# An early-fusion model on one core: merged transfers, one second encoder layer for both halves, keys turned by narrow products, and fill products of 128 columns

## The chip, the cores and the metric

The kernel runs on one core of one Trainium2 chip. The metric is the device time of one execution in microseconds. Before the change three timed executions took 3369.94, 3370.55 and 3380.7 us, median 3370.55.

## What is computed

Sixteen images and sixteen texts go through a tokenizer, two layers and an LSTM, all in float32. Cut to its core:

```
h = tokenizer(x)                       # 2x2 convolution, attention over 441 tokens of 256
h = concat([h, txt])                   # 16 sequences x 569 positions x 256
h = h + window_attention(layernorm(h)) # shifted windows of 64, 8 heads
h = h + top2_experts(layernorm(h))     # 8 experts, 256 -> 512 -> 256, gelu
# layer 1, attention: x = layernorm(h)
kp = tanh(gelu(x @ Wk1 + bk1) @ Wk2 + bk2) * freq * pi   # 64 key phases
qp = tanh(gelu(x @ Wq1 + bq1) @ Wq2 + bq2) * freq * pi   # 64 query phases
V  = x @ Wv + bv
memory    = cumsum(exp(i*kp)[..., None] * V[:, :, None, :], axis=1)
retrieved = real(sum(memory * exp(-i*qp)[..., None], axis=2)) / sqrt(pos * 64)
h = h + layernorm(retrieved) @ Wo + bo
# layer 1, feed-forward: y = layernorm(h)
xp = y @ W_ih.T + b_ih + b_hh
for t in range(569):
    gates = xp[:, t] + h_t @ W_hh.T;  i, f, g, o = split(gates)
    c = sigmoid(f) * c + sigmoid(i) * tanh(g);  h_t = sigmoid(o) * tanh(c)
# a gated prefix and suffix sum over the states, added to h
```

The LSTM's 569 steps depend on each other; nothing of one step can start before the state of the step before.

## The kernel before

**First part (0 to about 950 us).** Tokenizer, window attention and routing run as interleaved streams. Rows are normalised, routed, and scattered into `XS` by indirect DMAs (`send`, L904-916), two for each chunk of 128 rows. The list of places `at` (L899) stands in the pool `wk` of this part.

**Expert stage (about 950 to 1577 us).** `experts` (L1090-1265) computes which expert each of 79 tiles of 256 rows belongs to (`where`, L1139 and L1149). `weights` (L1165) loads an expert's packed weights (1154 KB) and `load` (L1171) the rows `xs`; the first two tiles' weights are issued ahead of everything (`ahead`, just below). Both stand in the pool `mo`. Four streams of tiles share TensorE. Beside them `prepare` (L1001-1077) loads what the next stage needs and clears buffers, among them the two `XO` buffers on GpSimd (L1044).

**Flow stage (about 1577 us to the end).** The sequence is cut into 10 blocks: one of 32 positions, eight of 64, one of 25 (`BLOCKS`). `fronts` and `backs`, two streams each, prepare the input of the LSTM, always two pairs of sequences a stream:

- `front` (L1340): adds the experts' rows to `h`, normalises, turns it, the encoders' first layers (`ek`, `eq`), the values `v`, and the encoders' second layer `z`. `Wk2` and `Wq2` are held twice side by side (`l1["Wk2"]`, [128, 2, 2, 64]), so that a product yields the 64 phases twice, in rows 0-63 (for the cosine) and 64-127 (for the sine). There are 36 fronts.
- `back` (L1474): scores `sc` of keys with queries, the keys turned by a whole-array transpose (L1490), `r` = retrieved, `ds` = what is added to the state, the output product `po`, the rows stored to `HF` (L1571), and the input projection `xm` with `Wih`, whose result `xp` is stored to `XCD` (three gates) and `XOD` (output gate) in DRAM (L1596, L1600). There are 36 backs with scores' turning and 4 late ones.

The steps of the recurrence (`steps`, L1661) read those stores back: `load` (inside it, L1671) fetches a unit of 8 positions, one DMA for `XC` and four for the four quarters of `XO`, each into 16 of the 32 rows of a quarter; the other 16 rows stay zero. A step then is: copy of the input into the PSUM banks `gates` and `out_gate` (L1690, L1695), products with `W_hh` (L1741, L1750), tanh of the gates (L1762, L1770), clearing the banks by a product of zeros (L1684), cell and state on VectorE (L1777 to L1805), tanh of the cell (L1798). `all_sums` does the prefix sums behind it.

**What sets the order.** Every f32 product of the fill work goes through `product`, which cuts the 128 output rows into four products of 32 rows[...]:

```
for m in range(0, out.shape[0], 32):
    own = slice(m, min(m + 32, out.shape[0]))
    nc.tensor.matmul(out[own], lhsT[:, own], rhs, start=start, stop=stop)
```

The order of TensorE, VectorE, ScalarE and GpSimd is written out while the program is built, by a planner (class `Order`). Each stream yields pieces with an engine and a cost, such as `yield "PE", 256 * COLUMN` (0.43 us); the recurrence has a table of its own costs (`STEP`). At each point the planner takes the recurrence's next step or a piece of fill work that fits in front of it, with an allowance `spare` of 0 to 0.45 us that depends on how far the backs of the next block are. Each engine then runs its list in order. A block's load waits, in the planner and on the chip, for all four backs of that block. The DMAs of SP are not in this order: the framework places them.

Of the kernel before, what the change touches and what calls it, by code (L numbers as in the profile page):

```python
# [10 lines left out]
F32 = mybir.dt.float32  # L11
BF16 = mybir.dt.bfloat16
AF = mybir.ActivationFunctionType
# [37 lines left out]
STEPS = 8  # L51
# [48 lines left out]

UNITS = np.arange(D).reshape(4, 2, 32).transpose(1, 0, 2).reshape(-1)
# [13 lines left out]
TURN = 0.11  # L115
# [179 lines left out]
def kernel(ctx: ExitStack, tc: tile.TileContext, a: dict, out: bass.AP):  # L295
# [489 lines left out]
    def routing():  # L785

        for p, lo, hi in PARTS:
# [111 lines left out]
            at = wk.tile([128, 2, n], mybir.dt.int32, name=f"at{u}", tag="at", bufs=3)  # L899
# [53 lines left out]
    XOD = [dram.tile([4, NB, n, 64], F32, name=f"XOD{j}") for j, (_, n) in enumerate(BLOCKS)]  # L953
# [35 lines left out]
    for n in ("Wk2", "Wq2"):  # L989
        l1[n] = l1w.tile([128, 2, 2, 64], F32, name=n)  # L990
# [10 lines left out]
    def prepare(mo):  # L1001
# [3 lines left out]
        def kxn(n):  # L1005
            return a[n].rearrange("(k p) n -> p k n", p=128)
# [9 lines left out]
        for n in ("Wk2", "Wq2"):  # L1016
            for i in range(2):
                nc.sync.dma_start(l1[n][:, :, i, :], kxn(n))
# [25 lines left out]
        for t in XO:  # L1044
            yield "POOL", 0.5
            nc.gpsimd.memset(t.rearrange("p t x -> p (t x)"), 0.0)
# [46 lines left out]
    def experts(g, mo, slots):  # L1093
# [71 lines left out]
        def weights(j, e=None):  # L1165
            e = planned(1, j, j + 1, E - 1)[0] if e is None else e
            w = mo.tile([128, WPACK], F32, name=f"w{g}_{j}", tag="w", bufs=bufs)
            nc.sync.dma_start(w, a["wpack"][bass.ds(e, 1)].rearrange("e p n -> (e p) n"))
            return w
# [169 lines left out]
    def front(p, c, n, at, slot):  # L1339
# [33 lines left out]
        for name in ("k", "q"):  # L1373
            e = bank(f"e{name}{u}", slot).rearrange("p (k n) -> p k n", k=2)
            g[name] = wk.tile([128, 2, 256], F32, name=f"g{name}{u}", tag=f"g{name}{slot}")
            for oc in range(2):
                for k in range(2):
                    yield "PE", 256 * COLUMN
                    product(
                        e[:, oc, :], l1[f"W{name}1"][:, k, oc * 128 : (oc + 1) * 128],  # L1380
                        xT[:, k, :], start=(k == 0), stop=(k == 1),
                    )
            for oc in range(2):
                yield "ACT", 0.46, "gelu"
                nc.scalar.activation(
                    g[name][:, oc, :], e[:, oc, :], AF.Gelu, bias=col(f"b{name}1", oc)
                )
# [8 lines left out]
        for j in range(2):  # L1396
            for k in range(2):
                yield "PE", 256 * COLUMN
                product(
                    v[:, j, :], xT[:, k, j * 128 : (j + 1) * 128], l1["Wv"][:, k, :],  # L1400
                    start=False, stop=(j + k == 2),
                )
        yield "DVE/ACT", 0.69, 0.58
        copy(V[:, both, :], v)
        z = bank(f"z{u}", slot).rearrange("p (k n) -> p k n", k=2)
        y = wk.tile([128, 2, 256], F32, name=f"fy{u}", tag=f"xn{slot}")
        for i, name in enumerate(("k", "q")):
            for k in range(2):
                yield "PE", 256 * COLUMN
                product(  # L1410
                    z[:, i, :], l1[f"W{name}2"][:, k].rearrange("p i x -> p (i x)"),
                    g[name][:, k, :], start=(k == 0), stop=(k == 1),
                )
        for i, name in enumerate(("k", "q")):
            yield "ACT", 0.45
            nc.scalar.activation(y[:, i, :], z[:, i, :], AF.Tanh, bias=col(f"b{name}2"))
# [31 lines left out]
    def add_to_state(p, c, u, slot, S2, kT, V, at):  # L1448

        for s in range(2):  # L1450
# [6 lines left out]
            for j in range(2):  # L1457
                yield "PE", 256 * COLUMN
                rhs = own[:, j, :] if c == 8 else V[:, at + j, :]
                product(  # L1460
                    ds[:, j, :], kT[0 if c == 8 else s][:, j, :], rhs, start=True, stop=True
                )
# [9 lines left out]
    def back(p, c, batch, at, slot, late=False):  # L1472
# [12 lines left out]
        for j in range(2):  # L1485
            yield "PE", 128 * COLUMN
            product(sc[:, j, 0, :], key[j], query[j], start=True, stop=True)
            if not late:
                yield "PE", TURN, "all"
                nc.tensor.transpose(sc[:, j, 1, :], key[j], ident)  # L1490
# [35 lines left out]
        for j in range(2):  # L1526
            yield "PE", 256 * COLUMN
            product(r[:, j, :], w[:, j, :], V[:, at + j, :], start=True, stop=not reads)
            if reads:
                yield "PE", 0.43  # L1530
            for s in range(2 if reads else 0):
                half = slice(64 * s, 64 * s + 64)
                product(
                    r[half, j, :], query[j][:, half], S2[:, s, j, :], start=False, stop=True
                )
        if not late:
            plan.fork(add_to_state(p, c, u, slot, S2, kT, V, at))
# [14 lines left out]
        for j in range(n):  # L1552
            for k in range(2):
                yield "PE", 256 * COLUMN
                product(
                    po[:, j, :], nT[:, k, j * 128 : (j + 1) * 128], l1["Wo"][:, k, :],
                    start=False, stop=(j + k == n),
                )
# [8 lines left out]
        for j in range(2):  # L1567
            for s in range(2):
                b = 2 * j + s
                src = h[32 * b : 32 * b + m, 0, :] if c8 else h[64 * s : 64 * s + m, j, :]  # L1570
                nc.sync.dma_start(HF[block][2 * p + b], src)  # L1571
# [6 lines left out]
        for i in range(2 * n):  # L1578
            j, half = i // 2, i % 2
            mm = bank(f"xm{u}_{i}", slot)  # L1580
            for part in range(2):
                for k in range(2):
                    yield "PE", 256 * COLUMN
                    at_ = 512 * half + 256 * part
                    product(
                        mm[:, 256 * part : 256 * part + 256], xT[:, k, j * 128 : (j + 1) * 128],
                        Wih[:, k, at_ : at_ + 256], start=(k == 0), stop=(k == 1),
                    )
# [4 lines left out]
            each = 32 if c8 else 64  # L1593
            for b in range(128 // each):
                own, seq = slice(each * b, each * b + m), 2 * (p + j) + b
                nc.sync.dma_start(  # L1596
                    XCD[block][4 * half : 4 * half + 4, seq].rearrange("a t x -> t a x"),
# [3 lines left out]
                    XOD[block][2 * half : 2 * half + 2, seq].rearrange("q t x -> t q x"),  # L1601
# [62 lines left out]
    def steps():  # L1664
# [7 lines left out]
        def load(k):  # L1672
# [5 lines left out]
            for q in range(4):  # L1678
                nc.sync.dma_start(XO[k % 2][32 * q + NB : 32 * q + 32, :n, :], XOD[j][q, :, u : u + n, :])
# [135 lines left out]
    def sums_of(r, j, u, n, X):  # L1815
# [8 lines left out]
        for k in range(2):  # L1824
            yield "PE", NB * n * COLUMN
            product(
                logit.rearrange("p (t b) -> p t b", b=NB), wl[:, k, :], X[:, k],
                start=(k == 0), stop=(k == 1),
            )
# [70 lines left out]
    with tc.manual_schedule(engines=ENGINES):  # L1900
        mo = tc.alloc_tile_pool(name="moe", bufs=1)
        for g in range(NG):
            plan.run(experts(g, mo, 4) + [prepare(mo)])
        mo.release()
        tiling.release()
# [170 lines left out]
```

## Time and profile before

| what | value |
|---|---|
| timed executions | 3369.94, 3370.55, 3380.7 us |
| the profiled execution's own time | 3360.87 us |
| its span in the profile | 3359.0 us |
| mean granted TensorE clock | 0.978 |
| DMA moved, mean | 366.81 MB, 109 GB/s |
| first part, to the last scattered row | 0 to about 956 us |
| expert stage, first to last product | 972.8 to 1576.3 us |
| recurrence, first to last `th` (L1798) | 1712.7 to 3316.2 us |
| stores `XCD`, `XOD` outside the late backs | 288 each |
| loads `xo` | 284 |

How to read it: a row of a group or of a timeline names the line, the engine, the operation, what it writes and reads, and how often; in brackets stands the engine's idle time ahead of it and who ended it. Each f32 matmul of the program is two records in the trace, with a weight load each, and the four products of one `product` call run side by side. The busy time of TensorE counts modelled ends and isn't a measure of how full it is. The chain of waits lists what released what, back from the end, in order of time with start and length; "SPq" is the time that SP's queue takes to issue a DMA, "DMA" the time from the issue to the landing.

### The profile page before, as it was taken

To read this page: it belongs to the slowest core of one execution; us is meant where nothing else is said; L and a number is where in the kernel's file an instruction comes from. 1 tells how busy PE (TensorE), PEld (TensorE's weight loads), DVE (VectorE), ACT (ScalarE), POOL (GpSimd) and SP (SyncE) were. 2 spreads that over 40 slices of the span, in tenths; PEclk is the share of its full clock that TensorE was granted. 3 is DMA by queue.
4 is the path that set the end of the run, shared out by engine and by line. 5 is a ranking of instruction groups with operands and counts; after the bars stand their busy time and mean duration, and the time that the engine had idled before them with its cause. 6 is when DMAs were issued, how large, how long until landed. Compare 5 with 4: busy or idle time off the path is not lost.

```text
span 3359.0 us, 134328 instructions
## 1 busy us (share of the span) xinstructions
PE 3055.1 (91%) x57536; PEld 2231.5 (66%) x57536; DVE 2027.2 (60%) x6787; ACT 1471.9 (44%) x5030; POOL 786.6 (23%) x1524
## 2 busy tenths in 40 slices
PE   5999999999859999997899999999999999999884
PEld 3666666666548888886566676766666666666652
DVE  4677777766732222222566777777777777766555
ACT  3545545454412222221444555555555555554442
POOL 1243554445533322232311001010101010100000
PEclk9999999999979999998999999999999999999997
DMA  5111221111176666664333333333333333333333
GB/s 180 53 46 57 89 79 54 55 38 41 42 251 234 220 231 225 225 229 141 100 100 88 90 82 86 84 94 78 97 77 92 84 93 79 76 91 80 90 103 113
DMA packets 276070, 366.81 MB, mean 109 GB/s; under 512 B 144480, under 2 KB 220176, under 8 KB 263312
## 3 DMA queue, kind: packets, MB, share of 16 engines
q1 hardware_dynamic: 249360, 300.91, 30.5%
q0 software_dynamic: 14496, 39.75, 3.1%
q10 hardware_dynamic: 11616, 17.56, 1.8%
q8 instruction: 451, 7.39, 0.9%
q14 instruction: 147, 1.20, 0.1%
HBM read 239.33 MB, written 118.75 MB: 107 GB/s over the span
## 4 chain that ended last, share of the span: by engine, by line
PE 37%; DVE 7%; ACT 5%; issue 2%; SPq 1%; DMA 1%; POOL 0%; ACTq 0%; DVEq 0%; POOLq 0%
PE gates L1741 13%; PE xm_False L1085 5%; PE out_gate L1750 2%; PE ek L1085 2%; PE po_False L1085 2%; PE z L1085 2%; PE v L1085 2%; PE eq L1085 2%; PE ds_False L1085 2%; ACT act L1762 1%; PE r_False L1085 1%; ACT th L1798 1%; DVE ab L1777 1%; DVE cT L1790 1%; DVE act L1783 1%
## 5 line engine op out<-in xcount | busy, mean ns | idle before, releaser
L1741 PE MATMUL gates<-W_hh,X 128*16 128x96 f32 (+1 forms) x18176 | 487.9, 248 | 63.9 <-DVE X L1805 61.6
L1741 PEld LDWEIGHTS gates<-W_hh,X 128*16 128x16 f32 (+1 forms) x18176 | 373.6, 103 | 258.5 <-DVE X L1805 245.0
L1248 ACT ACTIVATE hT<-hp,w 128x256 f32<-128x256 f32 x316 | 132.6, 472 | 481.5 <-PE hp L1241 314.5
L1762 ACT ACTIVATE act<-gates 128x96 f32<-128x96 f32 x568 | 142.1, 250 | 444.1 <-PE gates L1741 437.0
L1255 PE MATMUL y<-w,hT 128*128 128x256 f32 x1264 | 289.7, 382 | 5.2 <-ACT hT L1248 1.5
L1085 PE MATMUL xm_False<-W_ih,dxT_False 128*32 128x256 f32 x4352 | 292.3, 380 | 2.3 <-DVE dxT_False L1271 1.9
L1241 PE MATMUL hp<-xt,w 128*128 128x256 f32 x1264 | 287.6, 381 | 1.0 <-ACT hT L1248 1.0
L1777 DVE SCALAR_TENSOR_TENSOR ab<-act 128x64 f32<-128x64 f32 x568 | 127.9, 225 | 258.2 <-ACT act L1762 250.8
L1255 PEld LDWEIGHTS y<-w,hT 128*128 128x128 f32 x1264 | 236.8, 190 | 45.2 <-ACT hT L1248 14.4
L1684 PEld LDWEIGHTS <-nil 128*32 128x32 bf16 x4552 | 190.3, 94 | 111.0 <-issue 53.0
L1241 PEld LDWEIGHTS hp<-xt,w 128*128 128x128 f32 x1264 | 239.9, 191 | 35.7 <-ACT hT L1248 1.5
L1184 POOL DMA_INDIRECT YT<-ys,to x158 | 153.4, 971 | 440.4 <-DVE ys L1261 408.9
L1261 DVE TENSOR_TENSOR ys<-y,w 128x512 f32<-128x512 f32 x79 | 54.6, 691 | 316.3 <-PE y L1255 241.1
L1750 PE MATMUL out_gate<-W_hh,X 128*32 128x64 f32 x9088 | 233.8, 219 | 0.7 <-issue 0.7
L1690 ACT COPY gates<-xc 128x96 f32<-128x96 f32 x569 | 138.6, 244 | 182.0 <-DMA xc<-XCD 75.4
L1750 PEld LDWEIGHTS out_gate<-W_hh,X 128*32 128x32 f32 x9088 | 187.9, 110 | 2.9 <-issue 1.1
L1805 DVE SCALAR_TENSOR_TENSOR X<-toT,th 128x32 f32<-128x32 f32 x569 | 109.9, 193 | 120.5 <-ACT th L1798 116.9
L1798 ACT ACTIVATE th<-cT 128x32 f32<-128x32 f32 x569 | 130.5, 229 | 92.9 <-DVE cT L1790 43.1
L1301 POOL TENSOR_SCALAR d_False_rstd<-d_False_mv 128x2 f32<-128x2 f32 (+1 forms) x36 | 9.0, 250 | 671.8 <-DVE d_False_mv L1293 547.4
L908 POOL DMA_INDIRECT XS<-XN,at x144 | 149.1, 1035 | 45.6 <-issue 24.6
L693 PE MATMUL wqk<-wxT,wqkv 128*128 128x128 f32 x1152 | 150.6, 278 | 8.9 <-ACT wxT L687 8.6
L693 PEld LDWEIGHTS wqk<-wxT,wqkv 128*128 128x128 f32 x1152 | 139.4, 192 | 24.9 <-ACT wxT L687 13.5
(356 smaller groups left out, 6497.9 us busy)
## 6 DMA issues: line engine op xcount, KB each, us to landing
w<-in_wpack SPq DMA_DIRECT2D x79, 1154.0 KB
taps<-in_taps SPq DMA_DIRECT2D x16, 1764.0 KB
xc<-XCD SPq DMA_DIRECT2D x71, 384.0 KB
XCD<-xp_False SPq DMA_DIRECT2D x256, 96.0 KB
xs<-XS SPq DMA_DIRECT2D x79, 258.0 KB
yg<-YT SPq DMA_DIRECT2D x72, 256.0 KB
HD<-h SPq DMA_DIRECT2D x72, 128.0 KB
fh<-HD SPq DMA_DIRECT2D x72, 128.0 KB
```

The lines of the kernel that those rows point to most:

```text
L693: nc.tensor.matmul(qk[:, j, m, :], wqkv[:, k, D * j + 128 * m : D * j + 128 * m + 128], xT[:, k, :], start=(k == 0), stop=(k == 1),)
L908: fill(0, nc.gpsimd.indirect_dma_start(out=XS[0], out_offset=bass.IndirectOffsetOnAxis(ap=at[:, i, c - lo : c - lo + 1], axis=0), in_=XN[p ...
L1085: nc.tensor.matmul(out[own], lhsT[:, own], rhs, start=start, stop=stop)
L1184: keep(nc.gpsimd.indirect_dma_start(out=YT, out_offset=bass.IndirectOffsetOnAxis(ap=to[:, i : i + 1], axis=0), in_=ys[:, i, :], in_offset= ...
L1241: nc.tensor.matmul(hp[:, i, :], w1[:, k, hc * 128 : (hc + 1) * 128], xT[:, k, :], start=(k == 0), stop=(k == 1),)
L1255: nc.tensor.matmul(y[:, i, :], hT[:, hc, 128 * i : 128 * i + 128], w2[:, hc, :], start=(hc == 0), stop=(hc == 3),)
L1684: nc.tensor.matmul(g[32 * q : 32 * q + 32, :n], nil[:, :32], nil[:, :n], start=True, stop=last)
L1741: nc.tensor.matmul(GC[32 * q : 32 * q + NB * (1 + half), :96], before[:, kk, NB * (1 - half) :], Whh[:, kk, own : own + 96], start=False, ...
L1750: nc.tensor.matmul(GO[32 * q : 32 * q + 32, :64], before[:, kk, :], Whh[:, kk, own : own + 64], start=False, stop=(kk == 1),)
L1762: nc.scalar.activation(act[:, :96], GC[:, :96], AF.Tanh, scale=0.5), begun.pop((k, t))
L1777: nc.vector.scalar_tensor_tensor(ab, act[:, :64].rearrange("p (g x) -> p g x", g=2), 1.0, act[:, 64:].rearrange("p (g x) -> p g x", g=2), ...
L1798: nc.scalar.activation(th.rearrange("p k x -> p (k x)"), cT, AF.Tanh, scale=0.5)
```

## The change

- `XOD` gets a second half for each quarter, [4, 2, 16, n, 64], whose first half is filled with zeros once, by ten DMAs from `zeros` in `prepare`; the clearing of `XO` is gone. A unit's `XO` is then one load of 128 rows.
- A back stores `HF` in one DMA (the late ones still in four), and each `xp` in one DMA to `XCD` and one to `XOD`, instead of one for each sequence.
- The encoders' second layer is computed once: `Wk2` and `Wq2` stand side by side in one tile `W2`, the 64 key phases land in rows 0-63 of `z` and the 64 query phases in rows 64-127, the products of both encoders side by side; four tanh of 64 rows, instead of two of 128, write each result into both halves of `y`.
- The keys are turned by `product` with the identity instead of a transpose.
- The fill products `ek`, `eq`, `v`, `z`, `ds`, `r`, `po`, `xm` run over 128 columns at a time instead of 256; the logits `fin` over 8 positions (128 columns).
- The experts' weights stand in a pool of their own, `mw`, allocated ahead of `mo`, and `at` moves to the pool `xnp`.

```diff
-            at = wk.tile([128, 2, n], mybir.dt.int32, name=f"at{u}", tag="at", bufs=3)
+            at = xnp.tile([128, 2, n], mybir.dt.int32, name=f"at{u}", tag="at", bufs=3)
...
-    XOD = [dram.tile([4, NB, n, 64], F32, name=f"XOD{j}") for j, (_, n) in enumerate(BLOCKS)]
+    XOD = [dram.tile([4, 2, NB, n, 64], F32, name=f"XOD{j}") for j, (_, n) in enumerate(BLOCKS)]
...
-        for t in XO:
-            yield "POOL", 0.5
-            nc.gpsimd.memset(t.rearrange("p t x -> p (t x)"), 0.0)
+        for t in XOD:
+            i = -(-t.shape[3] // 16)
+            x = 32 * t.shape[3] // i
+            nc.sync.dma_start(
+                t[:, 0].rearrange("q b t x -> q (b t x)").rearrange("q (r i x) -> q r i x", r=32, i=i),
+                zeros.rearrange("p i x -> p (i x)")[:, :x].unsqueeze(1).to_broadcast([128, i, x]),
+            )
...
-            w = mo.tile([128, WPACK], F32, name=f"w{g}_{j}", tag="w", bufs=bufs)
+            w = mw.tile([128, WPACK], F32, name=f"w{g}_{j}", tag="w", bufs=bufs)
...
-                for k in range(2):
-                    yield "PE", 256 * COLUMN
-                    product(
-                        e[:, oc, :], l1[f"W{name}1"][:, k, oc * 128 : (oc + 1) * 128],
-                        xT[:, k, :], start=(k == 0), stop=(k == 1),
-                    )
+                for part in PARTS_OF:
+                    for k in range(2):
+                        yield "PE", 128 * COLUMN
+                        product(
+                            e[:, oc, part], l1[f"W{name}1"][:, k, oc * 128 : (oc + 1) * 128],
+                            xT[:, k, part], start=(k == 0), stop=(k == 1),
+                        )
...
-        for i, name in enumerate(("k", "q")):
-            for k in range(2):
-                yield "PE", 256 * COLUMN
-                product(
-                    z[:, i, :], l1[f"W{name}2"][:, k].rearrange("p i x -> p (i x)"),
-                    g[name][:, k, :], start=(k == 0), stop=(k == 1),
-                )
-        for i, name in enumerate(("k", "q")):
-            yield "ACT", 0.45
-            nc.scalar.activation(y[:, i, :], z[:, i, :], AF.Tanh, bias=col(f"b{name}2"))
+        for part in PARTS_OF:
+            for k in range(2):
+                yield "PE", 128 * COLUMN
+                for i, name in enumerate(("k", "q")):
+                    product(
+                        z[64 * i : 64 * i + 64, part], l1["W2"][:, k, i, :], g[name][:, k, part],
+                        start=(k == 0), stop=(k == 1),
+                    )
+        for i, name in enumerate(("k", "q")):
+            own = slice(64 * i, 64 * i + 64)
+            for half in (i, 1 - i):
+                yield "ACT", 0.45
+                nc.scalar.activation(
+                    y[64 * half : 64 * half + 64, i, :], z[own], AF.Tanh,
+                    bias=col(f"b{name}2", 0, own.start, own.stop),
+                )
...
-                yield "PE", TURN, "all"
-                nc.tensor.transpose(sc[:, j, 1, :], key[j], ident)
+                yield "PE", 128 * COLUMN
+                product(sc[:, j, 1, :], key[j], ident, start=True, stop=True)
...
-        for j in range(2):
-            for s in range(2):
-                b = 2 * j + s
-                src = h[32 * b : 32 * b + m, 0, :] if c8 else h[64 * s : 64 * s + m, j, :]
-                nc.sync.dma_start(HF[block][2 * p + b], src)
+        if late:
+            for b in range(4):
+                nc.sync.dma_start(HF[block][2 * p + b], h[32 * b : 32 * b + m, 0, :])
+        else:
+            nc.sync.dma_start(
+                HF[block][2 * p : 2 * p + 4].rearrange("(j s) t d -> (s t) j d", j=n), h
+            )
...
-            each = 32 if c8 else 64
-            for b in range(128 // each):
-                own, seq = slice(each * b, each * b + m), 2 * (p + j) + b
+            each, first = 4 // n, 2 * (p + j)
+            for own, seqs in (
+                [(slice(32 * b, 32 * b + m), slice(first + b, first + b + 1)) for b in range(each)]
+                if late else [(slice(0, 128), slice(first, first + each))]
+            ):
                 nc.sync.dma_start(
-                    XCD[block][4 * half : 4 * half + 4, seq].rearrange("a t x -> t a x"),
+                    XCD[block][4 * half : 4 * half + 4, seqs].rearrange("a s t x -> (s t) a x"),
...
-            for q in range(4):
-                nc.sync.dma_start(XO[k % 2][32 * q + NB : 32 * q + 32, :n, :], XOD[j][q, :, u : u + n, :])
+            nc.sync.dma_start(
+                XO[k % 2][:, :n, :], XOD[j][:, :, :, u : u + n, :].rearrange("q z b t x -> (q z b) t x")
+            )
...
-        for k in range(2):
-            yield "PE", NB * n * COLUMN
+        for t0 in range(0, n, STEPS):
+            steps_ = slice(t0, min(t0 + STEPS, n))
+            for k in range(2):
+                yield "PE", NB * min(n, STEPS) * COLUMN
...
+        mw = tc.alloc_tile_pool(name="moe_w", bufs=1)
         mo = tc.alloc_tile_pool(name="moe", bufs=1)
```

The products of `v`, `r`, `ds`, `po` and `xm` are cut in the same way as those of `ek`.

## What the change was predicted to do

> **What bounds the kernel now.** I read the page first (engine shares and costliest groups), then the starts of the recurrence's `th` activation (L1798) as a clock of the LSTM steps, then the timeline and the chain of waits at the places where that clock stops.
>
> TensorE is busy 91% by the page, but a busy TensorE is not a full one. The two rows below say who waits: the weight loads of the gate products (L1741) waited 245 us for `X`, the recurrence's own state, and the copy that begins a step (L1690) waited 75.4 us for `xc`, the stored input of the next block.
>
> ```profile
> PE 3055.1 (91%) x57536; PEld 2231.5 (66%) x57536; DVE 2027.2 (60%) x6787; ACT 1471.9 (44%) x5030; POOL 786.6 (23%) x1524
> L1741 PEld LDWEIGHTS gates<-W_hh,X 128*16 128x16 f32 (+1 forms) x18176 | 373.6, 103 | 258.5 <-DVE X L1805 245.0
> L1690 ACT COPY gates<-xc 128x96 f32<-128x96 f32 x569 | 138.6, 244 | 182.0 <-DMA xc<-XCD 75.4
> ```
>
> A bare step, where nothing else is left to do, takes 2.50 us from one gate product to the next (timeline of TensorE near the end, start and length in us):
>
> ```profile
> 3311.69 0.85 PE L1741 MATMUL gates<-W_hh,X 128*16 128x96 f32 x32 [0.41 <-DVE X L1805]
> 3312.36 0.41 PE L1750 MATMUL out_gate<-W_hh,X 128*32 128x64 f32 x16
> 3314.19 0.85 PE L1741 MATMUL gates<-W_hh,X 128*16 128x96 f32 x32 [0.41 <-DVE X L1805]
> ```
>
> `th` runs 569 times, from 1712.7 to 3316.2 us: 1603.5 us for 568 steps, where 568 x 2.50 = 1420. So 183 us are lost. By the starts of L1798, seven gaps ahead of a new block hold most of it: 57.7 us (step 32, 1796.4 to 1854.1), then 13.4, 19.1 and four times 15.9; steps stretched to 2.6-3.1 us hold most of the rest. A period of one block is 178 us (2568 to 2746) against 64 x 2.50 = 160. What happens in such a gap (ACT row; then the chain of waits):
>
> ```profile
> 2563.87 0.24 ACT L1690 COPY gates<-xc 128x96 f32<-128x96 f32 x1 [10.40 <-DMA xc<-XCD]
> ```
> ```profile
> 2552.35 0.70 DVE xp_False L1591
> ...
> 2557.73 0.61 SPq L1596
> ...
> 2558.39 0.62 SPq L1600
> ...
> 2561.10 4.43 DMA xo<-XOD
> ```
>
> The next block's input projections (`xm`, then `xp`) are finished too late, their stores leave SP's queue one by one at 0.6 us, and the loads follow. TensorE does fill work through the whole gap: the fill was not done in time. Why not, shows in one step in the middle of a block:
>
> ```profile
> 2438.26 0.85 PE L1741 MATMUL gates<-W_hh,X 128*16 128x96 f32 x32 [0.61 <-DVE X L1805]
> 2438.93 0.41 PE L1750 MATMUL out_gate<-W_hh,X 128*32 128x64 f32 x16
> 2439.48 0.23 PE L1684 MATMUL gates<-nil 128*32 128x96 bf16 x4
> 2439.68 0.21 PE L1684 MATMUL out_gate<-nil 128*32 128x64 bf16 x4
> 2439.70 1.06 PE L1085 MATMUL xm_False<-W_ih,dxT_False 128*32 128x256 f32 x16
> ```
>
> A fill product is 0.43 us (`xm` x32 = four products in 1.73 us in the chain of waits). The hole between the last out-gate product and the clearing of the gates is about 0.3 us and stays empty.
>
> [...] each f32 matmul leaves two records; in the chain of waits 32 records of 256 columns take 1.73 us, 0.216 us for each four that run side by side; 32 of 96 columns 0.66 us (0.083); 16 of 64 columns 0.22 us (0.055). That is a straight line with nearly no constant, so four of 128 columns are 0.109 us. [...] two narrow score products and two whole-array key transposes take from 2559.14 to 2560.25, 1.11 us, of which the products are 2 x 0.22. [...] `xs` issued at 964.92 behind 2.3 MB of weights is first used at 972.78.
>
> **The change, part by part.** *Second layer once.* `z` now is 4 x 0.43 = 1.73 us a front, half of it computing the same rows twice; afterwards half as many rows are computed, 0.86 us: 0.865 saved in each of 36 fronts, 3.5 a block. It adds two tanh of 64 rows a front, 72 x 0.47 us (row L1416) = 34 us, on ACT, which is 54% busy in this stage; if that cover is gone it costs up to 0.9 us of a front's latency, four fronts a block. Its first piece now waits for both encoders instead of one, with other streams' pieces in order behind it; but `z` comes after `v`, and its row names `V` leaving the bank as what it waited for (2.7 us in all), so I take nothing.
>
> *Keys by narrow products.* 1.11 us become four products of 0.22, 0.87: 0.25 saved in each of 36 backs, 1 us a block.
>
> *128 columns.* Streaming is unchanged; some 3,000 groups of four become 6,000 of 0.109. The loads of weights double. They lie beside the products: the out-gate's groups carry the same 128x32 loads every 0.055 us. Cost taken: none; its bound above is the third rival. The gain is packing. In the 178 us period TensorE needs: L1085, 1568 records, of which 1472 of 256 columns: 368 x 0.216 = 79.5, scores and biases 3.4; some 72 transposes at 0.14 (estimate from the rows above) 10; recurrence 64 x (0.66 + 0.22 + 0.07) = 61. Sum 154, so 24 us or 0.37 a step stay empty. A half product (0.217) fits in most steps: 64 x 0.2 = 13 at best, nothing at worst; I take half, 6.5. With 4.5 of work gone a block shrinks by 11; by up to 17.5 (160 is the floor), by 4.5 if nothing is packed better.
>
> *Merged transfers.* A back issues 16 stores of 0.61 and 4 of about 0.7 (chunk 8's: 0.43 and 0.5); afterwards 8 and 1, over 128 rows, such as the loads `fh` (0.45) show. A unit's four `xo` loads of 0.42 become one, with half its rows zero: 128 KB more for each of 71, 9 MB in 1600 us, nothing beside 90 GB/s. The one load waits for both halves of the stores where two of the four waited for one half; behind it on SP stand the loads of the next fronts, which now also queue less. In a steady block this lies beside other work; at a gap, from the end of the last `xp` at 2556.4 to `xo` at 2565.5, 9.1 us: four stores 2.6, loads 2.0, landing 4.4. Afterwards two stores 1.0, their landing about 1.9 that no longer hides under later issues, two loads 0.8, landing 3 to 4.4: some 7. This 2 us is taken inside the 11, since work and not the queue sets the period. Next late is again the fill.
>
> *Up to block 1 (1578 to 1849).* TensorE is the bound: its gaps sum to 33 us, 16 of them at the start. Ten `z` save 8.7, ten pairs of keys 2.5. After `xp` is done at 1697.4 SP still issues until 1706, the first step waits until 1711.5, and TensorE, in order, stands from 1709.0 to 1712.0 behind a clear: 3. After the last `xp` (1841.6) stores and loads take until 1851.9; half as many issues give 4 back. Packing in 32 steps, 3. Sum 21 (14 to 30).
>
> *Early weights.* `where` is known at 951.2, the first two weights start at 963.4, since they wait for memory of the first part; `xs` behind them at 964.9, TensorE at 972.8. Afterwards two weights start near 953. But DMA is full from 940 to 960 (share 0.92 to 1.08), with scatters and zeros that `xs` must wait for. I take 2 us, bounds 0 and 8. `at` elsewhere costs nothing.
>
> *Zeros.* Two memsets leave POOL; ten stores onto SP add 4 x 16 x 569 x 64 x 4 B = 9.3 MB. They depend on nothing but `zeros`, and SP's order isn't hand-written. I take nothing: the first part (DMA share 0.08 to 0.22 from 100 to 900 us) or the expert stage (0.67) can cover them. Uncovered, at 400 GB/s (965 to 980), 23 us. The split logits and merged `W2` tile change no time that I can see.
>
> *Sum.* 2 + 21 + 6 gaps x 11.5 (11 and half a microsecond of landing) = 69 + 3 in the last blocks = 95. The profiled execution took 3360.9 (span 3359.0 and 1.9 around it), giving 3266; it lies 9.7 below the median of 3370.55, and the forecast is for a median: **3276**.
>
> **The rivals.** (a) *Nothing is packed better*: the planner in the kernel finds the holes unusable, or too few pieces are ready (steps with no fill in mid-block speak for it). Left: 2 + 18 + 6 x 4.5 + 2 = 49: 3322. (b) *The gaps close*: 6 x 17.5 + 28 + 5 + 3 = 141: 3230. For it: work needs 149.5 of 160. (c) *Zeros ahead of the weights*: SP already lets the loads `lin` to `Wk1` (937.5 to 940.7) pass ahead of the weights; nine megabytes there cost 23: 3299. (d) *Slower: doubled weight loads bound the narrow products.* One load's mean is 110 ns; if four of 128 columns took more than 0.109 + 95/6000 = 0.125 us the gain is gone; at 0.14, 6,000 x 0.031 = 186 more: 3462. Against it: the same loads at 0.055.
>
> **How the numbers follow.** Forecast 0.52, (a) 0.2, (b) 0.12, (c) 0.08, (d) 0.05, no difference 0.03. 0.3%, about 10 us, is what a measurement here can tell from no change. Range: leaving out (d), no change and the outer edges of (a) and (b), 3222 to 3336. Faster 0.91, same 0.04, slower 0.05.
>
> **What would show it.** Right: periods of 164 to 169 us for blocks now 178, gaps under 8 us, `z` at 32 records of 128 columns, 0.109 us for each four records; first `th` near 1700 and step 32's gap under 48. Wrong: gaps as long as before (packing), first expert tile after 975 (zeros), steps over 2.6 us in most of a block (narrow products, or ACT).

## The result, and the profile after

The changed kernel takes **3544.47 us** (median of 5 runs, 3537.14 to 3548.1); the kernel before takes 3370.55 beside it. The ratio is 1.0504, 95% interval 1.0491 to 1.0516: 5% slower, where 3276 was forecast. The profiled execution has a span of 3541.4 us at a granted clock of 0.974.

The page of the changed kernel, the rows that answer to those of before:

```profile
PE 3065.3 (87%) x70184; PEld 2512.2 (71%) x70184; DVE 2021.0 (57%) x6769; ACT 1521.4 (43%) x5120; POOL 785.5 (22%) x1522
q8 instruction: 549, 8.99, 1.1%
L1764 PEld LDWEIGHTS gates<-W_hh,X 128*16 128x16 f32 (+1 forms) x18176 | 410.1, 103 | 185.3 <-DVE X L1828 111.0
L1088 PE MATMUL xm_False<-W_ih,dxT_False 128*32 128x128 f32 x8704 | 321.6, 274 | 23.3 <-issue 20.8
L1773 PE MATMUL out_gate<-W_hh,X 128*32 128x64 f32 x9088 | 276.0, 220 | 29.5 <-issue 28.5
L1773 PEld LDWEIGHTS out_gate<-W_hh,X 128*32 128x32 f32 x9088 | 221.2, 110 | 37.6 <-issue 36.2
L1713 ACT COPY gates<-xc 128x96 f32<-128x96 f32 x569 | 138.3, 243 | 165.1 <-PE gates L1707 115.8
```

TensorE has 12,648 products more and as many weight loads, and is busy a smaller share of a longer span. The weight loads wait 111 us for the state `X` instead of 245, and the copy that begins a step waits for TensorE's clearing, no longer for `xc`. New is the releaser "issue", time in which the engine waited for nothing that the profile shows: 20.8 us ahead of `xm`, 28.5 ahead of the out gate's products, which follow the gates' products with nothing to wait for. In the page of before the out gate's row had 0.7.

A bare step is what it was, 2.50 us (timeline of TensorE near the end):

```profile
3493.90 0.85 PE L1764 MATMUL gates<-W_hh,X 128*16 128x96 f32 x32 [0.41 <-DVE X L1828]
3494.57 0.41 PE L1773 MATMUL out_gate<-W_hh,X 128*32 128x64 f32 x16
...
3496.40 0.85 PE L1764 MATMUL gates<-W_hh,X 128*16 128x96 f32 x32 [0.41 <-DVE X L1828]
```

By the starts of `th`, the recurrence runs from 1731.5 to 3500.9 us: 1769.4, where it was 1603.5. Only 168 of 568 steps take 2.5 us (415 before); nearly all the others take 2.6 to 4.8. The gaps ahead of the blocks did shrink in six of seven places (51.2, 3.5, 7.9, 5.8, 7.0, 17.8 and 2.7 us). The time came in inside the blocks, in the middle of runs of one product (timeline of TensorE):

```profile
2565.12 0.27 PE L1088 MATMUL r_False<-V,w_False 128*32 128x128 f32 x1
2565.74 0.31 PE L1088 MATMUL r_False<-V,w_False 128*32 128x128 f32 x4 [0.35 <-issue]
...
2568.25 0.62 PE L1088 MATMUL eq<-fxT,Wq 128*32 128x128 f32 x16
2569.49 0.53 PE L1088 MATMUL eq<-fxT,Wq 128*32 128x128 f32 x12 [0.62 <-issue]
```

`r` stops after one record, `eq` after sixteen, and goes on with the same operands after a pause. Counted over products and weight loads, such pauses lie 256 instructions apart or a multiple of that: 256 from 2565.74 to 2569.49. The DMA records name the cause: queue q8, "instruction", brings packets of 16,384 bytes, 549 of them; 70,184 products and 70,184 loads are 140,368 instructions, and 140,368 / 256 = 548. The kernel before has 451 packets for 115,072 / 256 = 449.5. So each packet is 256 of TensorE's instructions, by this count of 64 bytes each. Near the rows above packets start at 2563.40, 2566.94 and 2570.69; the pauses end at 2565.74 and 2569.49, 2.34 and 2.55 us after a start. From 1877 to 3078 us two packets start 3.88 us apart on average (median 3.75, a quarter of them under 3.51), and never less than 3.24. TensorE waits for its own program: the pauses of the recurrence sum to 213.6 us, counted as the next section says. A packet itself takes 1.0 us (median); what fills the rest of the time between two starts, no run shows.

**Theory 1** is this supply: 256 instructions don't arrive faster than in about 3.4 us (an estimate from the distances above), and a group of four products of 128 columns uses eight (four products, four loads) in 0.109 us, 13.6 ns each, as fast as they come. **Theory 2** is the prediction's rival (d), the weight loads of each group. **Theory 3**: another part of the change costs it.

### The profile page after: what moved, and what is told of

Read it like the earlier page. It is cut to its first block, busy times and chain, and to the rows that moved or that the text cites. A ratio compares the mean times of both kernels' runs of the same rounds, so it can differ in the third digit from the quotient of the medians.

```text
span 3541.4 us, 158973 instructions
## 1 busy us (share of the span) xinstructions
PE 3065.3 (87%) x70184; PEld 2512.2 (71%) x70184; DVE 2021.0 (57%) x6769; ACT 1521.4 (43%) x5120; POOL 785.5 (22%) x1522
## 4 chain that ended last, share of the span: by engine, by line
PE 40%; issue 6%; DVE 5%; ACT 3%; DMA 1%; POOL 0%; ACTq 0%; SPq 0%; DVEq 0%; POOLq 0%
PE gates L1764 12%; PE xm_False L1088 7%; PE out_gate L1773 3%; PE v L1088 2%; PE ek L1088 2%; PE eq L1088 2%; PE r_False L1088 2%; PE po_False L1088 2%; PE ds_False L1088 2%; ACT th L1821 1%; ACT act L1785 1%; PE z L1088 1%; PE fin L1088 1%; DVE ab L1800 1%; DVE cT L1813 1%
## 5 line engine op out<-in xcount | busy, mean ns | idle before, releaser
L1764 PE MATMUL gates<-W_hh,X 128*16 128x96 f32 (+1 forms) x18176 | 532.1, 248 | 105.4 <-DVE X L1828 59.7
L1764 PEld LDWEIGHTS gates<-W_hh,X 128*16 128x16 f32 (+1 forms) x18176 | 410.1, 103 | 185.3 <-DVE X L1828 111.0
L1088 PE MATMUL xm_False<-W_ih,dxT_False 128*32 128x128 f32 x8704 | 321.6, 274 | 23.3 <-issue 20.8
L1773 PE MATMUL out_gate<-W_hh,X 128*32 128x64 f32 x9088 | 276.0, 220 | 29.5 <-issue 28.5
L1088 PEld LDWEIGHTS xm_False<-W_ih,dxT_False 128*32 128x32 f32 x8704 | 247.0, 110 | 36.5 <-issue 31.8
L1773 PEld LDWEIGHTS out_gate<-W_hh,X 128*32 128x32 f32 x9088 | 221.2, 110 | 37.6 <-issue 36.2
L1707 PE MATMUL gates<-nil 128*32 128x96 bf16 x2276 | 161.3, 209 | 23.2 <-ACT act L1785 5.7
L1707 PE MATMUL out_gate<-nil 128*32 128x64 bf16 x2276 | 152.7, 195 | 7.6 <-issue 6.8
```

Source lines behind the costliest of these rows:

```text
L1707: nc.tensor.matmul(g[32 * q : 32 * q + 32, :n], nil[:, :32], nil[:, :n], start=True, stop=last)
L1764: nc.tensor.matmul(GC[32 * q : 32 * q + NB * (1 + half), :96], before[:, kk, NB * (1 - half) :], Whh[:, kk, own : own + 96], start=False, ...
L1773: nc.tensor.matmul(GO[32 * q : 32 * q + 32, :64], before[:, kk, :], Whh[:, kk, own : own + 64], start=False, stop=(kk == 1),)
```

## The experiments

The table gives the ratio to the kernel before with its 95% interval, and from each profile TensorE's products and loads, the recurrence (first to last `th`), and in it the sum of pauses. A pause here is the distance of two starts of TensorE's products, where it is over 0.23 us, both belong to one line with the same operands, and the later one waits for no semaphore; the ordinary distance of two starts is counted with it. The labels e1 to e12 are explained one by one below; e4 and e11 were run once, for their profiles, so that they have no ratio, and e4 stands below alone.

| kernel | ratio | instructions | recurrence us | pauses us |
|---|---|---|---|---|
| before | 1 | 115,072 | 1603.5 | 4.8 |
| changed | 1.0504 (1.0491 to 1.0516) | 140,368 | 1769.4 | 213.6 |
| e1 | 0.9963 (0.9949 to 0.9977) | 114,928 | 1588.8 | 16.1 |
| e2 | 1.0025 (1.0014 to 1.0037) | 113,920 | 1611.2 | 17.8 |
| e3 | 1.0638 (1.0620 to 1.0656) | 140,544 | 1827.2 | 206.2 |
| e5 | 1.0183 (1.0170 to 1.0197) | 114,928 | 1588.8 | 16.1 |
| e6 | 1.0186 (1.0172 to 1.0200) | 114,928 | 1585.7 | 13.0 |
| e7 | 0.9985 (0.9978 to 0.9992) | 114,928 | 1603.0 | 11.5 |
| e8 | 1.0253 (1.0237 to 1.0268) | 115,072 | 1608.5 | 9.6 |
| e9 | 0.9919 (0.9905 to 0.9932) | 114,928 | 1582.3 | 10.9 |
| e10 | 1.0162 (1.0147 to 1.0176) | 124,144 | 1670.7 | 88.2 |
| e11, before again | | 115,072 | 1609.8 | 7.7 |
| e12 | 0.9906 (0.9890 to 0.9923) | 114,928 | 1585.0 | 11.0 |

**e1: the split undone.**

```diff
-PARTS_OF = [slice(0, 128), slice(128, 256)]
+PARTS_OF = [slice(0, 256)]
...
-            for part in range(4):
+            for part in range(2):
```

> The changed kernel with its fill products back at 256 columns (z and the logits too), all else as changed. Theory 1 (TensorE's supply of instructions: 256 instructions cannot arrive in less than about 3.4 us, and products of 128 columns use them up as fast): about 12,000 products and 12,000 weight loads fewer, stalls in the middle of runs of one product below 10 us in all where they were 165, blocks of 164 to 178 us, 3280 to 3335 us in all. Theory 2 (each group of four is bounded by its weight loads): the same direction, but the groups of four of 128 columns in the changed kernel would then have to start more than 0.109 us apart, which they don't. Theory 3 (another part of the change costs it: the four tanh, the merged transfers, the zeros or the planner's order): over 3450 us.

Measured: 3363.36 us. The split alone is the ratio of two ratios, 1.0504 / 0.9963 = 1.054 (1.052 to 1.057 from the ends of both intervals), **181 us**, as is the difference of the two recurrences (1769.4 - 1588.8). The pauses that went sum to 213.6 - 16.1 = 197.5 with the ordinary distances in them. The page of e1:

```profile
q8 instruction: 450, 7.37, 0.9%
L1773 PE MATMUL out_gate<-W_hh,X 128*32 128x64 f32 x9088 | 236.6, 219 | 1.3 <-issue 1.3
```

The out gate's products wait 1.3 us for "issue", where the changed kernel had 28.5. Theory 1 is met on the direction and nearly on the pauses (16.1 us, where under 10 was expected). The time is above its 3335: the other parts give less than I had thought, which the later runs look into.

**e2: keys turned by transposes again, on top of e1.**

```diff
-                yield "PE", 128 * COLUMN
-                product(sc[:, j, 1, :], key[j], ident, start=True, stop=True)
+                yield "PE", TURN, "all"
+                nc.tensor.transpose(sc[:, j, 1, :], key[j], ident)
```

> As the one before, and the keys turned by the whole-array transpose again: some 1,000 instructions fewer, 1 us of TensorE a block more. Theory 1: where supply no longer bounds, within 10 us of the one before. Theory 3, if the narrow turning of the keys is what costs: 100 us or more below the one before.

Measured: 3387.25, 24 us over e1. With the narrow turning the kernel is faster; neither theory's number fits, and as the planner's order changes with it, how much of the 24 us is the turning's own stays open.

**e3: the split alone, on the kernel before**, with the same cuts as in the change (the logits `fin` stay whole), such as:

```diff
-                    yield "PE", 256 * COLUMN
-                    at_ = 512 * half + 256 * part
+                    yield "PE", 128 * COLUMN
+                    at_ = 512 * half + 128 * part
```

> The kernel before with only the fill products cut to 128 columns. Theory 1: slower, 3480 to 3620 us, fetches 3.4 to 3.5 us apart through the flow stage and stalls every 256 instructions, over 150 us in all. Packing as forecast in the prediction: 3290 to 3350 us. Theory 3: within 20 us of 3370.

Measured: 3593.95 us, 6.4% slower, as theory 1 had it (3480 to 3620), with 206.2 us of pauses. So the split is sufficient, and no other part is needed: theory 3 falls as the main cause.

**e4: the same columns in more instructions.** At the end of the recurrence nothing is left to fill, and each step carries one product that keeps TensorE busy.

```diff
-                        product(GO[:, :D], ident, Whh[:, 0, :D], start=True, stop=True)
+                        w = D if j < len(BLOCKS) - 1 else 64
+                        for x in list(range(0, D, w)) * 2:
+                            product(GO[:, x : x + w], ident, Whh[:, 0, x : x + w], start=True, stop=True)
```

> The kernel before with the filling product of the last two blocks' steps doubled: in block 8 (positions 480 to 543) two products of 256 columns a step, in block 9 (544 to 568) the same columns in eight products of 64. The columns streamed are the same, 0.87 us a step; the instructions of a bare step go from 144 to 240. Theory 1: steps of block 9 take about 240 x 13.5 ns = 3.2 us, with a stall every 256 instructions, those of the bare second half of block 8 stay at 2.5 to 2.7. Theory 2 (group floor): groups of 64 columns run 0.055 us apart as the out gate's do, and both halves take the same.

Measured: bare steps of block 8 stay at 2.50; the 25 steps of block 9 take 84.1 us, 3.36 each on average; all but the first are longer than 2.50. 3.36 / 240 = **14.0 ns an instruction**. The timeline of TensorE in block 9:

```profile
3296.18 0.77 PE L1741 MATMUL gates<-W_hh,X 128*16 128x96 f32 x27 [0.55 <-issue]
...
3297.58 1.10 PE L1085 MATMUL out_gate<-W_hh,ident 128*32 128x64 f32 x64
3298.49 0.21 PE L1684 MATMUL out_gate<-nil 128*32 128x64 bf16 x4
3298.66 0.50 PE L1741 MATMUL gates<-W_hh,X 128*16 128x96 f32 x10
3299.66 0.61 PE L1741 MATMUL gates<-W_hh,X 128*32 128x96 f32 x18 [0.50 <-issue]
...
3301.99 0.67 PE L1741 MATMUL gates<-W_hh,X 128*16 128x96 f32 x18
3303.14 0.43 PE L1741 MATMUL gates<-W_hh,X 128*16 128x96 f32 x11 [0.48 <-issue]
```

The filling product's 64 records run from 3297.58 to 3298.49, 0.057 us for each four: the groups themselves are not slowed, and theory 2 falls. In this stretch the pause stands in the gates' products and moves through them, since a step has 240 instructions and a block of instructions 256; it ends at 3296.18, 3299.66 and 3303.14, every 3.48 us. The first three pauses of the block, which end at 3285.21, 3289.23 and 3292.71, stand inside the added product. From each of these six to the next there are exactly 256 instructions: what stalls is whatever stands at the edge of a block of 256, not the added work as such.

**e10: `xm` alone cut**, on e1: is there a threshold?

```diff
-            for part in range(2):
+            for part in range(4):
```

> The changed kernel at 256 columns (the first experiment) with xm alone cut to 128 columns: some 1,020 instructions a block more, 11,300 in place of 10,300, where the full split has 13,000. Theory 1 with its threshold (14.0 ns an instruction: 11,300 make 158 us a block, under the 160 of the recurrence, so that only runs of xm inside a step meet the limit): 10 to 45 us more than the first experiment, 0.999 to 1.010. A cost in proportion to the added instructions (37% of the full split's 181 us): 60 to 75 us more, 1.014 to 1.019. If the smaller pieces pack better as the prediction had it: below the first experiment.

Measured: 3434.0 us, 71 over e1, and 88.2 us of pauses, 72 more than e1 (its profiled execution lies 18 us above its median). My threshold falls, the cost in proportion fits. The mean over a block (11,300 x 14.0 = 158 us) isn't what decides. Little is fetched ahead, as e4 shows, where the pauses begin in the second step of 240 instructions: a run of narrow products meets the limit by itself, though bare steps before it (144 instructions in 2.50 us) leave time over. In the changed kernel's blocks the mean too is over the 160 us of the recurrence: 13,000 x 14.0 = 182 us, and blocks 1 to 6 took 193 to 207.

**e5, e6: where the zeros go.** In e1 SP issues the zeros among the loads of the first images (timeline of SP's queue in e1):

```profile
26.72 10.84 SPq L1046 DMA_DIRECT2D XOD<-zeros  x1
39.21 9.05 SPq L338 DMA_DIRECT2D taps<-in_taps  x2
48.31 28.94 SPq L1046 DMA_DIRECT2D XOD<-zeros  x3
77.44 9.75 SPq L338 DMA_DIRECT2D taps<-in_taps  x1
```

e5 takes them from `XO`, cleared in the expert stage; e6 also puts the weights and `at` back in their old pools.

```diff
+        nc.gpsimd.memset(XO[0].rearrange("p t x -> p (t x)"), 0.0)
...
-                zeros.rearrange("p i x -> p (i x)")[:, :x].unsqueeze(1).to_broadcast([128, i, x]),
+                XO[0].rearrange("p t x -> p (t x)")[:, :x].unsqueeze(1).to_broadcast([128, i, x]),
```

e6 besides:

```diff
-            at = xnp.tile([128, 2, n], mybir.dt.int32, name=f"at{u}", tag="at", bufs=3)
+            at = wk.tile([128, 2, n], mybir.dt.int32, name=f"at{u}", tag="at", bufs=3)
...
-            w = mw.tile([128, WPACK], F32, name=f"w{g}_{j}", tag="w", bufs=bufs)
+            w = mo.tile([128, WPACK], F32, name=f"w{g}_{j}", tag="w", bufs=bufs)
```

> The changed kernel at 256 columns (the first experiment), with the ten stores of zeros taken from XO, which GpSimd clears in the expert stage, so that they can't leave ahead of that; the computation is the same. Theory Z (the 9.3 MB stand among the first images' loads and push the first part back by some 9 us): the experts begin 7 to 12 us earlier, some 0.25 to 0.3% below the first experiment (0.9963). Theory that the zeros are hidden: within 0.1% of it, and the expert stage may be up to 5 us longer.

> As the one before, and the experts' weights and the list of places back in their old pools. If the early weights cost (their first hidden product came 9 us after the first turned tile, against 5.2 before): 2 to 5 us less, some 0.1%. If they gain the 2 us of the prediction: 2 us more.

Measured: 3439.01 and 3439.99, 76 and 77 us over e1: a miss. The recurrence is about e1's; the expert stage, from the first turned tile to the last product, takes 693.8 us in e5's profile, 605.5 in e1's, 88 longer. The timeline of SP's queue in e5:

```profile
1105.01 0.33 SPq L1173 DMA_DIRECT2D w<-in_wpack  x1
1108.98 84.27 SPq L1048 DMA_DIRECT2D XOD<-xo  x10
```

The ten stores keep SP's queue for 84 us, 9.3 MB at 111 GB/s, and the next tiles' rows and weights stand behind them. TensorE stops (stretches of e5: start and end, length, TensorE busy with its instructions, and so on for the engines, then clock, DMA share and GB/s):

```profile
1000.00:1100.00 100.00, 99.42 (x479) 86.33 (x478) 22.77 (x81) 23.06 (x56) 26.85 (x51) 1.00 0.67 224
1100.00:1200.00 100.00, 23.43 (x114) 20.17 (x112) 6.46 (x21) 6.14 (x15) 13.43 (x25) 0.63 0.32 122
```

The DMA engines are less busy than in the stretch before, so it isn't all of them that are short. By the DMA records of SP's queue (q1), exactly four packets are in flight in 82% of the time from 1115 to 1190 us, each of 2,048 bytes and 84 ns by the median; from 1000 to 1100 us it is 9.4 on average, and sixteen in a quarter of the time. Four packets of 2,048 bytes each 84 ns are 98 GB/s, nearly the whole rate. Why four at a time, no run shows. e6 against e5 is no difference that a timing shows. The profiles show the early weights' effect: from `where` known to the first product `hp`, 31.0 us in e1 and 29.2 in e5, 25.9 in e6.

**e7: less work alone; e8: merged transfers alone**, both on the kernel before. e7 takes from the change these lines and the four tanh; e8 takes the transfers as the change's diff has them, with the late zeros of e5.

```diff
-    for n in ("Wk2", "Wq2"):
-        l1[n] = l1w.tile([128, 2, 2, 64], F32, name=n)
+    l1["W2"] = l1w.tile([128, 2, 2, 64], F32, name="W2")
...
-                yield "PE", TURN, "all"
-                nc.tensor.transpose(sc[:, j, 1, :], key[j], ident)
+                yield "PE", 128 * COLUMN
+                product(sc[:, j, 1, :], key[j], ident, start=True, stop=True)
```

> The kernel before with only the second layer computed once and the keys turned by narrow products, all at 256 columns. By the prediction's own terms 4.5 us a block and 11 us up to block 1: about 47 us less, 0.986. If the planner's order takes part of the saved work back as empty TensorE (theory P): a third of that or less, 0.995 to 1.0.

> The kernel before with only the merged transfers, the zeros stored late, 256 columns, the second layer computed twice, the keys turned by transposes, the weights as before. By the prediction's terms 7 us up to block 1 and 2 us a gap: about 20 us less, 0.994. Theory P (a gap is set by the fill, and the order decides its length): within 0.3% of 1, of either sign.

Measured: e7 3371.3, 5 us gained of the forecast 47. e8 3464.77, 85 us slower. The late zeros cost 75 by the timings of e5 over e1, and 88 by the length of the expert stage, in e8 against e11 (the kernel before, below) as in e5 against e1; so what the merged transfers give by themselves is within some 10 us of nothing, and the recurrence is as long as before. Theory P is met for e7. In e8, whose TensorE runs the same instructions in the same order as before (step by step, 8 of 13,201 fill records lie in another step), four gaps are 15.9 us long, as before, though the transfers are quicker. The timelines of ScalarE and of TensorE in e8 at the gap ahead of position 288, which begins at 2652.5:

```profile
2662.58 0.24 ACT L1711 COPY gates<-xc 128x96 f32<-128x96 f32 x1 [8.55 <-DMA xc<-XCD]
```
```profile
2664.63 0.64 PE L1092 MATMUL r_False<-V,w_False 128*32 128x256 f32 x8
2665.49 1.07 PE L1092 MATMUL z<-gk,Wk 128*32 128x256 f32 x16 [0.21 <-DVE V L1278]
2666.38 0.84 PE L1762 MATMUL gates<-W_hh,X 128*16 128x96 f32 x32
```

The copy comes 10.1 us into the gap (12.0 before), the first gate product 13.93 us (13.92 before): it stands behind fill on TensorE's list, and the copy's wait was covered. The distance is written into the plan: `plan.mark(("back", n, slot), 6.0)` (L1655 before) and `plan.mark(("loaded", k), 4.0)` (L1680) allow 10 us from the last `xp` to the step, and in the gaps whose last `xp` came late the first gate product started 8.5 to 10.7 us after it in the kernels so far with 256 columns, with one exception of 12.2 in e7. With 128 columns pauses come on top, and it was up to 12.6.

**e9: e1 without the zeros and the early weights; e11: the kernel before again**, for the chip that e9 and e10 ran on. e9 on e1:

```diff
-            nc.sync.dma_start(
-                XO[k % 2][:, :n, :], XOD[j][:, :, :, u : u + n, :].rearrange("q z b t x -> (q z b) t x")
-            )
+            for q in range(4):
+                nc.sync.dma_start(XO[k % 2][32 * q + NB : 32 * q + 32, :n, :], XOD[j][q, :, u : u + n, :])
```

> The changed kernel at 256 columns, and without the zeros and the early weights: XOD, its four loads a unit and the clearing of XO on GpSimd as in the kernel before; kept of the change are the merged stores, the second layer once and the narrow turning of the keys. Theory Z (the zeros stand ahead of the first images' loads and cost some 9 us, the early weights some 3): ratio 0.990 to 0.994, experts beginning where the kernel before begins them. If the zeros and weights cost nothing: 0.996, as the first experiment. The flow stage's 284 narrow loads instead of 71: 0 to 3 us more.

> The kernel before, unchanged, profiled on the chip of the two runs beside it, since the first part of these runs began its experts up to 11 us later than the profile of before although nothing in it was changed. If that is the chip's own: experts' rows known at 962 to 968 us, not 951, and the recurrence as long as before, 1603 us.

Measured: **3352.03 us, 0.9919**. Against e1's 0.9963 the zeros, the early weights and the single `XO` load cost 0.44%, 15 us. e11 knew the experts' places at 965.3 us and has a recurrence of 1609.8: the first part's delay against the first profile (951.2) is the chip's. On the chip of e1 the two kernels with an unchanged first part (e3, e4) knew them at 962.2 and 962.1, e1 at 971.3: 9 of the 15 lie there. Yet e9, without zeros there, had them 4 us after e11, so I can't divide the 9 further. The other 6 are the recurrence's (1588.8 in e1, 1582.3 in e9), no more than the kernel before differs between two profiles on different chips (1603.5 and 1609.8).

**e12: a shorter allowance in the plan**, on e9.

```diff
-            plan.mark(("back", n, slot), 6.0)
+            plan.mark(("back", n, slot), 4.0)
...
-            plan.mark(("loaded", k), 4.0)
+            plan.mark(("loaded", k), 3.0)
```

> The run without zeros and early weights, with two of the planner's estimates lowered: 4.0 us in place of 6.0 from a back's last piece to its stored input, 3.0 in place of 4.0 for a unit's load. In the gaps of every run so far the first gate product starts 8.5 to 10 us after the last xp, to a hundredth of a microsecond the same with merged transfers and without (13.92 us into the gap in both), which is the 10 us of these two estimates and not the transfers. Theory G (the gap is an allowance of the plan, so merged transfers alone can't shorten it): the distance from the last xp to the first gate product falls to 6 or 7 us where xp is late, and the whole by 8 to 20 us, 0.986 to 0.9895. Theory W (the fill that stood in the gap is needed and now stretches steps): gaps shorter, the whole within 5 us of 0.9919. Theory D (the transfers need the 10 us): the same distance, with TensorE idle in it.

Measured: 0.9906, not told apart from e9. Four late gaps take 12.6 to 14.9 us. The distance is 7.7 to 8.7 us there, not 6 or 7: the copies are only 0.3 us ahead of the product, and TensorE stood idle 0.6 to 1.7 us for them, which it did in no gap of e9. So theory D holds in part, the transfers now bind. The recurrence is no shorter, as theory W has it; that what stood in the gaps stretches steps elsewhere fits, but no run shows it by itself.

## Why the prediction was wrong

- **The step that failed** is the one on 128 columns: "Streaming is unchanged; some 3,000 groups of four become 6,000 of 0.109. The loads of weights double", and "Cost taken: none". It was costed in columns and in loads; what doubled was the fill's instructions, and their supply was near its limit. The term put at nothing is 181 us by e1. The sign for it lay in the page of before, in the row of q8, which I passed over; its columns are packets, MB and share:

```profile
q8 instruction: 451, 7.39, 0.9%
```

  From 1854 to 2924 us its packets were 4.37 us apart on average (median 4.11), each with 256 instructions. At the 14.0 ns of e4 a packet's instructions need 3.58 us: 82% of the supply was in use, and the split takes a block from 10,448 instructions to some 13,000, a quarter more. I didn't divide.
- The rival (d) had the direction and a price of 0.14 us a group. The groups are 0.109 apart when fed; spread over some 6,360 groups (twice the 25,440 added instructions / 8) the 181 us are 0.028 each, so the price was right for a wrong reason. Its counter-argument, "the same loads at 0.055", looked at four groups in a row, 32 instructions, too few to use up a block of 256.
- **Packing**, 46 of the 95 us (the forecast less case (a)): in the changed kernel a block leaves 46 to 48 us of TensorE without columns by the prediction's way of counting (21.5 before). The gaps after the first went to 2.7 to 7.9 in five of six places, as packing would make them. In e3 only two of them shrank (to 6.6 and 3.3; the others took 16.3 to 24.6), so that smaller pieces pack better isn't shown; what is shown is that TensorE couldn't be fed with them.
- **Up to block 1**: forecast 21, of which 3 by packing. From the last expert's scatter to block 1's first step e9 takes 260.4 us, e11 279.0: 18.6 gained. Right.
- **The gaps without packing**: 4.5 each, 27 in all, forecast. From block 1's first step to block 7's e9 takes 1057.0, e11 1075.0: 18, two thirds. The last blocks give nothing (3 forecast). With 2 for the weights, which e9 doesn't have, that is case (a), 49; e9 measured 27 by the timings and 32 by the profiles. Neither the work nor the merged stores give it alone: TensorE's instructions stand in the same order in e8 as in the kernel before, and in e9 as in e7. In the first order merged stores leave the recurrence as it was (1608.5 against 1609.8 in e11), in the second they take it from 1603.0 to 1582.3. The traces show what the single stores hold up there. In the gap at step 32, 57.8 us in e7 and 50.2 in e9, the addition that writes `xp` (L1596 of e7) waited 8.0 us for a store of the same buffer to `XOD`, and TensorE's scores 5.6 us for that addition; in e9 the addition waited for no store. In the next four gaps of e7 the first gate product waited 0.1 to 1.2 us for the copy, in e9 in none.
- **What a gap waits for** was misread. The row of the copy, 10.40 us behind `xc`, is true, but little hung on the copy: the first gate product came 1.9 us after it in the kernel before and 3.8 us after it in e8, at the same place; the 2 us taken for quicker transfers don't exist in that order, which is written out in advance.
- **Early weights**: 2 us gained was forecast, about 3 lost is what the profiles show. The weights start 1.8 us after `where`, as forecast; the rows `xs` start 17.5 us after it in e5, 12.8 in e6 (13.6 before). The last scatter, which they wait for, leaves GpSimd 12.4 us after `where` in e5 and 5.2 in e6, so the scatters are later beside the early weights; that the shared DMA is the reason is argued.
- **Zeros**: nothing was taken, with 23 us as the uncovered bound. The first part hid most; uncovered they cost 76 by the timings, at 111 GB/s: the rate taken, 400 GB/s, was that of transfers with more packets in flight (16 on average from 965 to 980 us).
- **The four tanh** at nothing: no run took them out alone, and ScalarE's share went from 44% to 45% in e9, which is faster.
- What would show it wrong was named rightly, "steps over 2.6 us in most of a block (narrow products...)"; its chance of 5% was far too small.

## What to carry to other kernels

When a product is cut into smaller pieces, count instructions as well as columns: divide the time of a stretch by the products and weight loads in it, and compare with the instruction queue's packets in the same trace (here one block of 256 in 3.4 to 3.6 us, 13 to 14 ns each; a block of the sequence took 17.1 ns an instruction before and 15.2 in the changed kernel). A pause with "issue" as its releaser in the middle of a run of one operation was the sign here (0.35 and 0.62 us in the rows above). In a kernel whose order is written in advance, a wait on one engine is worth something only if the engine that sets the pace waits for it: check how far behind the released instruction its successor starts (here 1.9 us before and 3.8 us in e8).

## What was not expected of the hardware

- TensorE's instructions came in blocks of 256, never closer than 3.24 us (median 3.75 in the changed kernel's middle, 3.51 in e4's last block), and in eight of ten cases a pause ended 2.3 to 2.8 us after a packet's start. In e4 the pauses began in the second step of 240 instructions after bare steps that needed less (144 in 2.50 us): no large reserve had been built up.
- Ten stores of zeros, 9.3 MB from a source that is repeated, kept SP's queue for 84 us at 111 GB/s while the DMA share fell to 0.32: four packets were in flight at a time, where other transfers had up to sixteen or more.
